# Expert outputs added to token rows in DRAM by accumulating indirect DMA, and a different order of the causal query tiles

## The chip, the core and the metric

The kernel runs on one core of one Trainium2 chip. A core has TensorE (PE in the profile, with the weight loads in a row of their own, PEld), VectorE (DVE), ScalarE (ACT), GpSimd (POOL) and SyncE (SP); each takes its instructions in program order and waits on semaphores. DMAs are issued by SP, ACT or POOL and are carried out by 16 DMA engines that all queues share. Time is device microseconds (us) for one execution, and the figure compared is the median over executions.

## The reference, cut to what matters

A two-layer decoder on `x` of 4 sequences x 512 tokens x 256 channels, with a context of 4 x 1024 x 128. Layer 0: a landmark attention, a causal self-attention with 16 heads plus a cross-attention to the context, and a linear layer with quantised operands. Layer 1: a hyperbolic attention, two attention blocks with an MLP each, and last a mixture of experts. Two parts matter here.

The causal attention of layer 0, 16 heads of width 16:

```python
att = jnp.einsum('bhqd,bhkd->bhqk', q, k) * scale
att = jnp.where(causal[None, None], att, -jnp.inf)
y = jnp.einsum('bhqk,bhkd->bhqd', jax.nn.softmax(att, axis=-1), v)
```

and the mixture of 8 experts, of which each token uses two:

```python
gate_scores = jax.nn.softmax(x @ Wg + bg, axis=-1)
topk_scores, topk_idx = jax.lax.top_k(gate_scores, TOP_K)
topk_scores = topk_scores / (jnp.sum(topk_scores, axis=-1, keepdims=True) + 1e-08)
...
for e in range(NUM_EXPERTS):
    h = jax.nn.gelu(x @ W1[e] + b1[e])
    y = h @ W2[e] + b2[e]
    output = output + y * combine_w[..., e:e + 1]
```

Here the `x` that enters the experts is a layernorm, and the result is added to the unnormalised `x`.

## The kernel before, in words

All arithmetic is in fp32 apart from a few bf16 helpers. `x` stays in SBUF as 16 tiles of 128 tokens from start to end. The stages follow each other in time as `l0_attn` and `context_T`, then `l0_xattn`, `l1_attn`, `l1_xattn`, and the experts (`Slots`), which begin while `l1_xattn` still runs.

*Order of the work.* The first two functions are ordered by a scheduler. From `l0_xattn` on the order is written by the kernel itself (`tc.manual_schedule()`): class `Stream` walks through steps. A step holds up to four "d" tiles (scores of one query tile for four heads, `d_tile`, L386; their row maxima on DVE, L394 for causal and L398 for full attention) and up to four "a" tiles of a unit some steps behind (transposed scores of one key tile, L421; exponentials on ACT, L422), and the products with the values (`outputs`, L517). In a step two d tiles and two a tiles are issued alternately, then the other two of each. The four heads of a unit lie in the four groups of 32 rows of the PE array. Everything else, such as projections, norms, the MLPs, the gate and the experts, hangs in `chains` of small pieces with a due step and a cost; `fill` lays them into the steps.

*Causal units.* A causal unit has four query tiles; tile `qt` needs (qt + 1) x 128 keys. `d_tile` takes them as `qt = NT - 1 - i`, so widths 512, 384, 256, 128 over its four steps. Key tile `kt` of an a tile needs the queries from kt x 128 on: widths 512, 384, 256, 128 as well. A unit's first a step lies ten steps after its first d step in the causal part, so that where both tiles of a step are causal, a step's d tile has index i + 2 (modulo 4) where its a tile has index i. Each of the four batches has 16 causal d steps; ten of them go with a tiles of a cross unit (always 512 wide) and six with causal ones.

*The gate.* For each batch, `gate` normalises `x` into `e.z` (a tile of the pool `z`), computes the scores, picks two experts (`choose`, `choose2`, `choose3`), counts each token's place within its expert (`rank`) and writes each token's normalised row twice, by `scatter`: eight indirect DMAs on POOL's queue (L1653) into the DRAM table `rows`, 2048 rows for each expert. Each of the eight waits for the one before it to land, since all of them write `rows`. `biases` and `biases2` add the experts' output biases, weighted, to `x`. `clear_rows` fills `rows` with zeros at the start of the kernel (L1554, 2 MB for each expert).

*The slots.* `NSLOT` = 39 slots of 128 rows each belong to one expert. Slots 0 to 15 (`NEARLY`) come from a table made after batch 2 (`table_early`), the others from one made after batch 3 (`table_late`). For a slot, `fetch_z` (L1803) loads 128 rows of `rows`, and `fetch_w` (L1809) loads one expert's whole weights, 2 MB, into one of four buffers; both are issued by SP after it has read the table. `turn` transposes the rows (L1820, L1822), `hidden` computes the first product (L1831) and the activation (L1833), `output` the second (L1838), which DVE copies out of PSUM to one of three `ys` buffers (L1840); SP stores it to the DRAM table `outs` (L1841). `round` fixes the order: fetch slot s+3, hidden s+1, turn s+2, output s. The second chain, `rest`, is made when batch 3 has been routed; its first piece is `fetch(16)`, which costs nothing in the planner and is therefore laid at once, among the fetches of slot 8. So on SP's queue stands the fetch of slot 16, rows first and then weights, ahead of the weights of slots 9 to 15, and its rows wait for the last scatter of batch 3.

*The end.* `places` (L1767 to L1794, on DVE, laid into the slots' work) computes for each token where its two results lie in `outs`. After the last slot, `end` gathers them: for each of the 16 token tiles two indirect DMAs on POOL's queue into `yk` (L1884), each followed by a multiply-add on DVE into `x` (L1887), and then a store of the tile on SP (L1888).

Of the kernel before, what the change touches and what calls it, by code (L numbers as in the profile page):

```python
# [13 lines left out]
I32 = mybir.dt.int32  # L14
# [16 lines left out]
VW = 16 * 17 + 15  # L31
NSLOT = 2 * B * T // P + E - 1

WROW = 2 * 1024 + 8 * C + 8
# [3 lines left out]
def decoder_kernel(ctx: ExitStack, tc: tile.TileContext, a: dict, out: bass.AP):  # L38
# [268 lines left out]
    class Stream:  # L307
# [70 lines left out]
        def d_tile(self, u, i, j):  # L378
            if u.mode == "causal":
                qt, hf = NT - 1 - i, 0  # L380
                n = (qt + 1) * P
            else:
                qt, hf, n = i // u.halves, i % u.halves, 512
            r = ts(j, 32)
            ps = ring()
            PE.matmul(ps[:, 0:n], u.qT[r, ts(qt)], u.kT[r, hf * 512 : hf * 512 + n], start=True, stop=True)  # L386
# [1129 lines left out]
    def moe_state(stack):  # L1516
        m = SimpleNamespace()
        pl = pool(stack, "moe", 1)
        dram = stack.enter_context(tc.tile_pool(name="moed", bufs=1, space=bass.MemoryType.DRAM))
        m.rows = dram.tile([E * B * T + P, C], F32, name="rows", tag="rows")  # L1520
        m.outs = dram.tile([NSLOT * P, C], F32, name="outs", tag="outs")
        m.wg = load(pl, "wg", rows("wg"), [P, 2, E])
# [15 lines left out]

        m.hot = pl.tile([P, 2, NTILE, E], BF16, name="hot", tag="hot")
        m.wt = pl.tile([P, 2, NTILE], F32, name="wt", tag="wt")  # L1540
# [9 lines left out]
    def clear_rows(m, pl):  # L1550
        zero = pl.tile([P, C], F32, name="zero", tag="zero")
        G.memset(zero, 0.0)
        for e in range(E):
            nc.sync.dma_start(  # L1554
                m.rows[ts(e, B * T), :].rearrange("(n p) c -> p n c", p=P), mid_bc(zero, B * T // P)
            )
        nc.sync.dma_start(m.rows[E * B * T :, :], zero)


    def gate(m, b, e, gs, hT, bank):  # L1560
# [8 lines left out]
        def z():  # L1569
            if not hasattr(e, "z"):  # L1570
                e.z = zpool.tile([P, NT, C], F32, name="ln_z", tag="ln_z")
            return e.z

        def begin():
            e.hT = hT()

        def flip(c):
# [16 lines left out]

        def top(mx, o):
            p, mc = e.p, t1("gmc")
            V.tensor_reduce(mx, p, AX.X, ALU.max)
            V.tensor_tensor(o, p, last_bc(mx, E), ALU.is_equal)
            V.tensor_mul(o, o, mid_bc(m.iw, NT))
            V.tensor_reduce(mc, o, AX.X, ALU.max)  # L1600
            V.tensor_tensor(o, o, last_bc(mc, E), ALU.is_equal)

        def choose():
            p = e.p
            e.o = [t8("go1"), t8("go2")]
            e.m2, e.sm = t1("gm2"), t1("gsm")
            V.tensor_reduce(e.sm, p, AX.X, ALU.add)
            V.reciprocal(e.sm, e.sm)
            V.tensor_mul(p, p, last_bc(e.sm, E))
            top(e.m1, e.o[0])  # L1610

        def choose2():
            p = e.p
            V.scalar_tensor_tensor(p, e.o[0], -2.0, p, ALU.mult, ALU.add)
            top(e.m2, e.o[1])

        def choose3():
# [4 lines left out]
            for k, mk in enumerate((e.m1, m2)):  # L1622
                V.tensor_mul(m.wt[:, k, ts(b, NT)], mk, sm)
                V.tensor_copy(m.hot[:, k, ts(b, NT), :], e.o[k])
            e.both = gs.tile([P, NT, E], BF16, name="gboth", tag="gboth")
# [24 lines left out]
        def scatter(t):  # L1650
            for k in range(2):
                i = b * NT + t
                G.indirect_dma_start(  # L1653
                    m.rows, bass.IndirectOffsetOnAxis(ap=m.idx[:, i, k : k + 1], axis=0), e.z[:, t, :], None
                )
# [13 lines left out]
        def biases2(h):  # L1669
            ps = bank()  # L1670
            for t in range(2):
                PE.matmul(ps[:, ts(t, C)], e.cT[:, ts(2 * h + t)], m.b2, start=True, stop=True)
            V.tensor_add(xb[:, ts(h, 2), :], ps.rearrange("p (t c) -> p t c", c=C), xb[:, ts(h, 2), :])

        return (
# [9 lines left out]
    class Slots:  # L1685
# [40 lines left out]
        def table(self, nm, nslot, end, less, plus):  # L1726
# [20 lines left out]
            V.tensor_copy(tab[:, 1, :], row)  # L1747
            return tab

        def table_early(self):  # L1750
            self.tab0 = self.table("tab0", NEARLY, self.end0, self.n0, None)

# [5 lines left out]
        def table_late(self):  # L1758
# [4 lines left out]

            self.tab1 = self.table("tab1", NSLOT - NEARLY, self.end1, less, n0[:, 0:1])


        def places(self):  # L1767
            m, one = self.m, self.st
            offs = []
            for nm, end, n, base in (("off0", self.end0, self.n0, 0), ("off1", self.end1, self.n1, NEARLY)):  # L1770
                off = self.t8(nm, E)
                V.tensor_sub(off, end, n)
                if base:
                    V.tensor_sub(off, off, self.n0)
                V.tensor_scalar(off, off, float(base), float(P), ALU.add, ALU.mult)
                V.tensor_sub(off, off, m.first)
                offs.append(off)
            V.tensor_sub(offs[0], offs[0], offs[1])
            lim = self.t8("lim", E)
            V.scalar_tensor_tensor(lim, self.n0, float(P), m.first, ALU.mult, ALU.add)  # L1780
            tmp = one.tile([P, NTILE, E], F32, name="tmp", tag="tmp")
            at, sel = (one.tile([P, NTILE], F32, name=n, tag=n) for n in ("slot", "early"))
            for k in range(2):
                V.tensor_mul(tmp, m.hot[:, k], mid_bc(lim, NTILE))
                V.tensor_reduce(sel, tmp, AX.X, ALU.add)
                V.tensor_tensor(sel, m.at[:, k, :], sel, ALU.is_lt)
                V.tensor_mul(tmp, m.hot[:, k], mid_bc(offs[0], NTILE))
                V.tensor_reduce(at, tmp, AX.X, ALU.add)
                V.tensor_mul(sel, sel, at)
                V.tensor_mul(tmp, m.hot[:, k], mid_bc(offs[1], NTILE))  # L1790
                V.tensor_reduce(at, tmp, AX.X, ALU.add)
                V.tensor_add(at, at, sel)
                V.tensor_add(at, at, m.at[:, k, :])
                V.tensor_copy(m.idx[:, :, k], at)  # L1794

# [3 lines left out]
        def fetch_z(self, u):  # L1799
            t, i = (self.tab0, u.s) if u.s < NEARLY else (self.tab1, u.s - NEARLY)  # L1800
            row = nc.sync.value_load(t[0:1, 1, i : i + 1], min_val=0, max_val=E * B * T)
            u.z = self.zp.tile([P, C], F32, name="zs", tag="zs")
            nc.sync.dma_start(u.z, self.m.rows[bass.ds(row, P), :])  # L1803
# [7 lines left out]
        def fetch(self, s):  # L1811
            u = self.us[s]
            if s >= NEARLY:
                self.fetch_z(u)
            self.fetch_w(u)

        def turn(self, u):
# [3 lines left out]
            u.zT = self.tp.tile([P, 2, P], F32, name="zsT", tag="zsT")  # L1821
            V.tensor_copy(u.zT, ps[:, 0:C].rearrange("p (c n) -> p c n", n=P))  # L1822

        def hidden(self, u, h):
# [10 lines left out]
        def output(self, u):  # L1835
# [3 lines left out]
            y = self.yp.tile([P, C], F32, name="ys", tag="ys")  # L1839
            V.tensor_copy(y, ps[:, 0:C])  # L1840
            nc.sync.dma_start(self.m.outs[ts(u.s), :], y)  # L1841

        def begin(self, stack):
            self.st = pool(stack, "l6c", 1)
            self.wp = pool(stack, "l6w", 4)
            self.zp = pool(stack, "l6z", NEARLY)
            self.tp = pool(stack, "l6t", 3)
            self.hp = pool(stack, "l6h", 2)
# [24 lines left out]
        def rest(self):  # L1873
            work = self.round(NEARLY - 3, NSLOT)
            work.insert(12, (0.5, self.places))
            return work


        def end(self):
            m = self.m  # L1880
            for i in range(NTILE):
                for k in range(2):
                    y = self.yp.tile([P, C], F32, name="yk", tag=f"yk{k}")
                    G.indirect_dma_start(  # L1884
                        y, None, m.outs, bass.IndirectOffsetOnAxis(ap=m.idx[:, i, k : k + 1], axis=0)
                    )
                    V.scalar_tensor_tensor(x[:, i, :], y, m.wt[:, k, i : i + 1], x[:, i, :], ALU.mult, ALU.add)  # L1887
                nc.sync.dma_start(out[i // NT, ts(i % NT), :], x[:, i, :])  # L1888

# [132 lines left out]
```

## Time and profile before

| | |
|---|---|
| median of 3 executions | 3517.08 us (3512.65 to 3517.96) |
| the profiled execution: its own time, and the span of its instructions | 3505.88 us, 3504.0 us |
| mean TensorE clock granted, of full speed | 0.914 |
| busy, share of the span: PE, PEld, DVE, ACT, POOL | 87%, 43%, 60%, 54%, 22% |
| weights of the slots: 39 loads of 2052 KB, issue to landing | 8.8 us (median) |
| store of a slot's output, 128 KB, issue to landing | 4.2 us (median) |
| scatter of 128 rows to `rows`, issue to landing | 2.4 us (median) |
| last product of the last slot ends, in the chain that ended last | about 3455 us |

How to read it: the page of a profile gives the busy time of each engine, and the chain of work that ended last, followed back from the last instruction. A busy share over the whole span is a mean over stages with different limits, so what a stage is bound by is read from that stretch. The profiled execution is one execution; it was 11 us faster than the median of the three others.

### The profile page before, as it was taken

How to read it: one execution, taken by the hardware profiler on the slowest of the kernel's cores; microseconds unless marked ns; L12 is line 12 of the kernel's file. 1: busy time of each engine (PE TensorE's matmuls, PEld its weight loads, DVE VectorE, ACT ScalarE, POOL GpSimd, SP SyncE). 2: the span in 40 equal slices, each digit the busy share in tenths (PEclk: the TensorE clock that was granted, in tenths of full speed). 3: DMA queues.
4: the chain of work that ended last, by engine and by line, in shares of the span. 5: the costliest groups of instructions: out<-in, count | busy, mean ns of one | idle time of the engine just before them, and what ended most of it. 6: DMA issues, size and time to landing. Idle time of an engine off the chain costs nothing.

```text
span 3504.0 us, 50650 instructions
## 1 busy us (share of the span) xinstructions
PE 3055.5 (87%) x19095; PEld 1489.4 (43%) x19095; DVE 2107.0 (60%) x5076; ACT 1901.9 (54%) x3845; POOL 781.5 (22%) x667
## 2 busy tenths in 40 slices
PE   6689999999998576677899999999998998987994
PEld 3433333333333344344434444433333333457894
DVE  4576676776765677876776565655646656532112
ACT  2235555454553865879587667465663655532231
POOL 1010112122022745677222121100102001011003
PEclk9789999999999567777899999999998999999997
DMA  8100000010001100110000000000000000045895
GB/s 281 59 24 7 1 7 3 6 31 4 11 19 41 56 1 32 54 69 7 25 1 1 1 19 1 7 13 19 13 1 13 7 1 19 1 164 208 290 328 168
DMA packets 81397, 176.08 MB, mean 50 GB/s; under 512 B 6264, under 2 KB 63744, under 8 KB 76032
## 3 DMA queue, kind: packets, MB, share of 16 engines
q1 hardware_dynamic: 76016, 161.16, 13.1%
q0 software_dynamic: 3072, 8.39, 0.8%
q8 instruction: 150, 2.46, 0.3%
q10 hardware_dynamic: 2064, 3.29, 0.3%
q14 instruction: 95, 0.78, 0.1%
HBM read 127.48 MB, written 45.34 MB: 49 GB/s over the span
## 4 chain that ended last, share of the span: by engine, by line
PE 66%; DVE 13%; ACT 7%; issue 7%; DMA 5%; POOL 2%; SPq 0%; ACTq 0%; DVEq 0%; POOLq 0%
PE ps_s L386 16%; PE ps_g L517 7%; PE ps_s L421 5%; PE ps_s L661 3%; PE ps_s L1831 3%; PE ps_s L1838 3%; PE ps_s L1410 3%; PE ps_s L1356 3%; PE ps_s L1426 3%; PE ps_s L414 2%; PE ps_s L1145 2%; PE ps_g L524 2%; DMA rows<-ln_z,idx 1%; PE ps_s L1367 1%; DMA we<-in_we 1%
## 5 line engine op out<-in xcount | busy, mean ns | idle before, releaser
L422 ACT ACTIVATE pt<-ps_s 128x512 f32<-128x512 f32 (+2 forms) x1536 | 791.0, 569 | 749.0 <-PE ps_s L421 647.8
L386 PE MATMUL ps_s<-kT,qT 32*128 32x512 f32 (+3 forms) x3072 | 921.9, 623 | 45.6 <-ACT pt L422 28.0
L398 DVE TENSOR_REDUCE mx<-ps_s 128x1 f32<-128x512 f32 x768 | 489.3, 683 | 222.0 <-PE ps_s L386 124.8
L386 PEld LDWEIGHTS ps_s<-kT,qT 32*128 32x128 f32 x3072 | 310.9, 186 | 338.5 <-issue 96.4
L390 DVE TENSOR_REDUCE mx<-ps_s 128x1 f32<-128x512 f32 x512 | 328.3, 684 | 194.1 <-PE ps_s L386 190.9
L421 PE MATMUL ps_s<-qa,kT 32*128 32x512 f32 (+3 forms) x1536 | 436.0, 590 | 4.9 <-ACT pt L422 3.1
L421 PE MATMUL ps_s<-qT,kT 32*128 32x512 f32 x1536 | 417.6, 636 | 0.0
L402 ACT ACTIVATE ps_s<-ps_s,mx 128x512 f32<-128x512 f32 x512 | 340.9, 670 | 32.8 <-DVE mx L390 32.3
L1833 ACT ACTIVATE hid<-ps_s,we 128x128 f32<-128x128 f32 x312 | 88.9, 368 | 221.4 <-PE ps_s L1831 144.5
L1105 POOL TENSOR_TENSOR s<-s,mh 128x1280 f32<-128x1280 f32 x64 | 187.1, 2948 | 76.9 <-ACT mh L1104 57.1
L394 DVE CUSTOM_DVE_ANT_0 junk<-ps_s,dmask 128x512 f32<-128x512 f32 (+3 forms) x256 | 125.2, 489 | 95.8 <-PE ps_s L386 52.9
L1831 PE MATMUL ps_s<-zsT,we 128*128 128x128 f32 x1248 | 148.8, 278 | 22.7 <-DMA we<-in_we 20.6
L1088 PE MATMUL ps_s<-qk 32*128 32x256 f32 (+3 forms) x512 | 105.3, 628 | 65.6 <-DVE mh L1093 55.3
L421 PEld LDWEIGHTS ps_s<-qa,kT 32*128 32x128 f32 x1536 | 143.8, 185 | 42.7 <-DVE mx L398 24.0
L414 PE MATMUL ps_s<-qm,all 3*128 3x512 bf16 x768 | 156.6, 387 | 5.8 <-ACT ps_s L402 3.1
L164 POOL TENSOR_TENSOR ln_r<-ln_ve,mhalf 128x4 f32<-128x4 f32 x40 | 40.8, 1020 | 538.4 <-DVE ln_ve L159 476.0
L1831 PEld LDWEIGHTS ps_s<-zsT,we 128*128 128x128 f32 x1248 | 146.5, 194 | 28.0 <-issue 19.2
L1120 POOL TENSOR_TENSOR s<-s 128x1280 f32<-128x1280 f32 x64 | 147.6, 2337 | 12.3 <-ACT s L1116 12.3
L1147 DVE COPY pt<-ps_s 128x512 f32<-128x512 f32 x160 | 108.3, 687 | 58.7 <-PE ps_s L1145 58.7
L1145 PE MATMUL ps_s<-ident,s 128*128 128x128 f32 x640 | 127.7, 336 | 16.6 <-ACT s L1139 15.3
L1838 PE MATMUL ps_s<-we,hid 128*128 128x256 f32 x624 | 141.0, 379 | 0.0
L1093 DVE TENSOR_SCALAR_CACHE_REDUCE mh<-ps_s 128x512 f32<-128x512 f32 (+3 forms) x256 | 108.5, 486 | 53.1 <-PE ps_s L1092 28.8
(439 smaller groups left out, 5117.5 us busy)
## 6 DMA issues: line engine op xcount, KB each, us to landing
we<-in_we SPq DMA_DIRECT2D x39, 2052.0 KB, 8.8
rows<-zero SPq DMA_DIRECT2D x8, 2048.0 KB, 16.8
qk_d<-qkT SPq DMA_DIRECT2D x32, 256.0 KB, 2.7
qk<-qk_d SPq DMA_DIRECT2D x8, 1024.0 KB, 6.5
zs<-rows SPq DMA_DIRECT2D x39, 128.0 KB, 3.6
outs<-ys SPq DMA_DIRECT2D x39, 128.0 KB, 4.2
li<-in_a_li SPq DMA_DIRECT2D x4, 1024.0 KB, 8.7
v_d<-vp SPq DMA_DIRECT2D x16, 143.5 KB, 1.8
```

Source lines behind the costliest of these rows:

```text
L386: PE.matmul(ps[:, 0:n], u.qT[r, ts(qt)], u.kT[r, hf * 512 : hf * 512 + n], start=True, stop=True)
L390: V.tensor_reduce(m, ps[:, 0:n], AX.X, ALU.max, negate=True)
L398: V.tensor_reduce(m, ps[:, 0:n], AX.X, ALU.max)
L402: S.activation(ps, ps, AF.Exp, bias=m, accum_out=sm)
L414: PE.matmul(ps, self.ones[r, :], u.qm[r, :], start=True, stop=False)
L421: PE.matmul(ps[:, c0:], u.kT[r, ts(kt)], (u.qa if u.first_row else u.qT)[r, c0:], start=u.first_row, stop=True)
L422: S.activation(u.pt[:, j, c0:], ps[:, c0:], AF.Exp, scale=u.scale)
L517: PE.matmul(o[r, c0:], u.v(kt, j), pt[:, j, c0:], start=first, stop=last)
L1105: G.tensor_add(s, s, m)
L1145: PE.transpose(ps[:, ts(j)], u.s[h // 2][:, h % 2, c0 : c0 + P], ident)
L1831: PE.matmul(ps[:, ts(f)], u.w[:, k : k + P], u.zT[:, c, :], start=c == 0, stop=c == 1)
L1838: PE.matmul(ps[:, 0:C], u.h[:, f, :], u.w[:, 2048 + f * C : 2048 + f * C + C], start=f == 0, stop=f == 7)
```

## The change

Rows carry four more numbers. `rows` gets `RW` = 260 columns: the token's number, its second weight, the difference of its two weights, and a mark that says which expert is its first. The gate writes them into its own tile `gz`, of the pool `l5g`, which takes the place of `e.z`; cleared rows get the number of a spare row. A slot then knows its rows' tokens and weights: `turn` has three more small DVE instructions, and `output` multiplies by the weight as it copies out of PSUM.

The results are summed in DRAM. A new table `sums` has one row for each token and 128 spare rows. After `biases2` POOL writes the batch's `x` into it, and each slot adds its 128 weighted rows by one indirect DMA on POOL's queue that accumulates. The program orders these DMAs: each waits for the one before it to land. `outs`, its stores, `places` and the gathers are gone; `end` copies `sums` to `out` by four DMAs from DRAM to DRAM, two on SP's queue and two on ACT's.

The fetch of slot 16 takes the weights first and then the rows. The causal query tiles are taken as 1, 0, 3, 2, so that widths are 256, 128, 512, 384. The buffers for the turned rows grow from three to four, since `turn`'s new small tiles are in the same pool.

The program's order on POOL's queue around batch 3 becomes: the adds of slots 0 to 4, the constants for the late table, the eight scatters, the add of slot 5, the write of batch 3 into `sums`, and the other 33 adds. On SP's queue the stores of `outs` are missing, and nothing else moves but slot 16's weights.

```diff
+RW = C + 4
...
-                qt, hf = NT - 1 - i, 0
+                qt, hf = (1 - i) % NT, 0
...
-        m.rows = dram.tile([E * B * T + P, C], F32, name="rows", tag="rows")
-        m.outs = dram.tile([NSLOT * P, C], F32, name="outs", tag="outs")
+        m.rows = dram.tile([E * B * T + P, RW], F32, name="rows", tag="rows")
+        m.sums = dram.tile([B * T + P, C], F32, name="sums", tag="sums")
...
+        num = pl.tile([P, NTILE + 1], I32, name="numi", tag="numi")
+        G.iota(num, pattern=[[P, NTILE + 1]], base=0, channel_multiplier=1)
+        m.num = pl.tile([P, NTILE + 1], F32, name="num", tag="num")
+        V.tensor_copy(m.num, num)
...
-        zero = pl.tile([P, C], F32, name="zero", tag="zero")
+        zero = pl.tile([P, RW], F32, name="zero", tag="zero")
         G.memset(zero, 0.0)
+        V.tensor_copy(zero[:, C : C + 1], m.num[:, NTILE:])
...
+        nc.sync.dma_start(m.sums[B * T :, :], zero[:, 0:C])
...
-                e.z = zpool.tile([P, NT, C], F32, name="ln_z", tag="ln_z")
+                e.zr = gs.tile([P, NT, RW], F32, name="gz", tag="gz")
+                e.z = e.zr[:, :, 0:C]
...
+            V.tensor_copy(e.zr[:, :, C], m.num[:, ts(b, NT)])
...
-                V.tensor_copy(m.hot[:, k, ts(b, NT), :], e.o[k])
+            V.tensor_copy(e.zr[:, :, C + 1], m.wt[:, 1, ts(b, NT)])
+            V.tensor_sub(e.zr[:, :, C + 2], m.wt[:, 0, ts(b, NT)], m.wt[:, 1, ts(b, NT)])
...
+            if h:
+                G.dma_start(m.sums[ts(b, T), :].rearrange("(t p) c -> p t c", p=P), xb)
...
-        def places(self):
...
         def fetch(self, s):
             u = self.us[s]
+            if s == NEARLY:
+                self.fetch_w(u)
             if s >= NEARLY:
                 self.fetch_z(u)
-            self.fetch_w(u)
+            if s != NEARLY:
+                self.fetch_w(u)
...
+            mark = self.mark0[:, u.s : u.s + 1] if u.s < NEARLY else self.mark1[:, u.s - NEARLY : u.s - NEARLY + 1]
+            u.to = self.tp.tile([P, 1], I32, name="to", tag="to")
+            V.tensor_copy(u.to, u.z[:, C : C + 1])
+            u.wt = self.tp.tile([P, 1], F32, name="wts", tag="wts")
+            V.tensor_tensor(u.wt, u.z[:, C + 3 : C + 4], mark, ALU.is_equal)
+            V.scalar_tensor_tensor(u.wt, u.wt, u.z[:, C + 2 : C + 3], u.z[:, C + 1 : C + 2], ALU.mult, ALU.add)
...
-            V.tensor_copy(y, ps[:, 0:C])
-            nc.sync.dma_start(self.m.outs[ts(u.s), :], y)
+            V.tensor_scalar_mul(y, ps[:, 0:C], u.wt)
+            G.indirect_dma_start(
+                self.m.sums, bass.IndirectOffsetOnAxis(ap=u.to, axis=0), y, None, compute_op=ALU.add
+            )
...
-            self.tp = pool(stack, "l6t", 3)
+            self.tp = pool(stack, "l6t", 4)
...
-            work.insert(12, (0.5, self.places))
...
         def end(self):
-            m = self.m
-            for i in range(NTILE):
-                for k in range(2):
-                    y = self.yp.tile([P, C], F32, name="yk", tag=f"yk{k}")
-                    G.indirect_dma_start(
-                        y, None, m.outs, bass.IndirectOffsetOnAxis(ap=m.idx[:, i, k : k + 1], axis=0)
-                    )
-                    V.scalar_tensor_tensor(x[:, i, :], y, m.wt[:, k, i : i + 1], x[:, i, :], ALU.mult, ALU.add)
-                nc.sync.dma_start(out[i // NT, ts(i % NT), :], x[:, i, :])
+            for b in range(B):
+                (nc.scalar if b % 2 else nc.sync).dma_start(out[b], self.m.sums[ts(b, T), :])
```

More of the change, by code (lines that the diff above doesn't have):

```diff
@@ L1537, in moe_state @@
         )
-        m.hot = pl.tile([P, 2, NTILE, E], BF16, name="hot", tag="hot")
+        num = pl.tile([P, NTILE + 1], I32, name="numi", tag="numi")
+        G.iota(num, pattern=[[P, NTILE + 1]], base=0, channel_multiplier=1)
+        m.num = pl.tile([P, NTILE + 1], F32, name="num", tag="num")
+        V.tensor_copy(m.num, num)
         m.wt = pl.tile([P, 2, NTILE], F32, name="wt", tag="wt")
@@ L1592, in scores, with top @@
             S.activation(e.p, e.p, AF.Exp)
-        def top(mx, o):
-            p, mc = e.p, t1("gmc")
+        def top(mx, o, mc):
+            p = e.p
             V.tensor_reduce(mx, p, AX.X, ALU.max)
@@ L1609, in choose @@
             V.tensor_mul(p, p, last_bc(e.sm, E))
-            top(e.m1, e.o[0])
+            top(e.m1, e.o[0], e.zr[:, :, C + 3])
         def choose2():
@@ L1614, in choose2 @@
             V.scalar_tensor_tensor(p, e.o[0], -2.0, p, ALU.mult, ALU.add)
-            top(e.m2, e.o[1])
+            top(e.m2, e.o[1], t1("gmc"))
         def choose3():
@@ L1653, in scatter @@
                 G.indirect_dma_start(
-                    m.rows, bass.IndirectOffsetOnAxis(ap=m.idx[:, i, k : k + 1], axis=0), e.z[:, t, :], None
+                    m.rows, bass.IndirectOffsetOnAxis(ap=m.idx[:, i, k : k + 1], axis=0), e.zr[:, t, :], None
                 )
@@ L1747, in table @@
             V.tensor_copy(tab[:, 1, :], row)
-            return tab
+            mark = self.t8(nm + "m", nslot)
+            V.tensor_scalar(mark, ex, -1.0, float(E), ALU.mult, ALU.add)
+            return tab, mark
         def table_early(self):
-            self.tab0 = self.table("tab0", NEARLY, self.end0, self.n0, None)
+            self.tab0, self.mark0 = self.table("tab0", NEARLY, self.end0, self.n0, None)
         def count_late(self):
@@ L1762, in table_late @@
             V.tensor_sub(less[:, 0 : E - 1], less[:, 0 : E - 1], n0[:, 1:E])
-            self.tab1 = self.table("tab1", NSLOT - NEARLY, self.end1, less, n0[:, 0:1])
-        def places(self):
[L1768 to L1782, printed above, removed]
-            for k in range(2):
[L1784 to L1794, printed above, removed]
+            self.tab1, self.mark1 = self.table("tab1", NSLOT - NEARLY, self.end1, less, n0[:, 0:1])
         def go(self):
@@ L1801, in fetch_z @@
             row = nc.sync.value_load(t[0:1, 1, i : i + 1], min_val=0, max_val=E * B * T)
-            u.z = self.zp.tile([P, C], F32, name="zs", tag="zs")
+            u.z = self.zp.tile([P, RW], F32, name="zs", tag="zs")
             nc.sync.dma_start(u.z, self.m.rows[bass.ds(row, P), :])
@@ L1839, in output @@
             y = self.yp.tile([P, C], F32, name="ys", tag="ys")
-            V.tensor_copy(y, ps[:, 0:C])
-            nc.sync.dma_start(self.m.outs[ts(u.s), :], y)
+            V.tensor_scalar_mul(y, ps[:, 0:C], u.wt)
+            G.indirect_dma_start(
+                self.m.sums, bass.IndirectOffsetOnAxis(ap=u.to, axis=0), y, None, compute_op=ALU.add
+            )
         def begin(self, stack):
-            self.st = pool(stack, "l6c", 1)
             self.wp = pool(stack, "l6w", 4)
             self.zp = pool(stack, "l6z", NEARLY)
-            self.tp = pool(stack, "l6t", 3)
+            self.tp = pool(stack, "l6t", 4)
             self.hp = pool(stack, "l6h", 2)
@@ L1873, in rest @@
         def rest(self):
-            work = self.round(NEARLY - 3, NSLOT)
-            work.insert(12, (0.5, self.places))
-            return work
+            return self.round(NEARLY - 3, NSLOT)
         def end(self):
-            m = self.m
-            for i in range(NTILE):
-                for k in range(2):
-                    y = self.yp.tile([P, C], F32, name="yk", tag=f"yk{k}")
-                    G.indirect_dma_start(
-                        y, None, m.outs, bass.IndirectOffsetOnAxis(ap=m.idx[:, i, k : k + 1], axis=0)
-                    )
-                    V.scalar_tensor_tensor(x[:, i, :], y, m.wt[:, k, i : i + 1], x[:, i, :], ALU.mult, ALU.add)
-                nc.sync.dma_start(out[i // NT, ts(i % NT), :], x[:, i, :])
+            for b in range(B):
+                (nc.scalar if b % 2 else nc.sync).dma_start(out[b], self.m.sums[ts(b, T), :])
     moe = moe_state(ctx)
```

## The prediction

> **What bounds the kernel now.** I read the page first, then busy times by stretch, then the chain that ended last in order of time, then TensorE's timeline in one causal stretch. The page says that the whole is a TensorE kernel:
>
> ```profile
> PE 66%; DVE 13%; ACT 7%; issue 7%; DMA 5%; POOL 2%; SPq 0%; ACTq 0%; DVEq 0%; POOLq 0%
> ```
>
> But the change lies mostly in the last 10% of the span, where the limits differ (columns: stretch, length, busy us and counts for PE, PEld, DVE, ACT, POOL; then clock, DMA share, GB/s):
>
> ```profile
> 3182.00:3227.00 45.00, 27.10 (x176) 24.13 (x174) 11.11 (x44) 6.84 (x24) 7.64 (x8) 0.89 0.57 218
> 3227.00:3292.00 65.00, 61.10 (x400) 55.88 (x400) 11.99 (x46) 18.25 (x64) 0.00 (x0) 0.97 0.72 258
> 3300.00:3448.00 148.00, 148.00 (x1030) 139.74 (x1029) 17.26 (x41) 46.79 (x164) 0.00 (x0) 1.00 0.86 311
> 3455.00:3504.00 49.00, 0.21 (x1) 0.00 (x0) 15.92 (x33) 0.00 (x0) 30.29 (x32) 0.55 0.47 131
> ```
>
> From 3300 PE is full, but the 16 DMA engines are at 0.86 as well. In the last 49 us PE does nothing. The chain tells what each stretch waits for (start, length, what):
>
> ```profile
> 3189.12 5.23 DMA rows<-ln_z,idx
> ...
> 3194.62 2.41 DMA rows<-ln_z,idx
> ...
> 3209.00 2.40 DMA rows<-ln_z,idx
> ...
> 3214.26 12.49 DMA we<-in_we
> 3226.89 5.67 PE ps_s L1831 x32
> ...
> 3284.73 0.42 DVE ys L1840
> 3286.63 0.30 DVE tmp L1784
> ...
> 3291.86 0.42 DVE zsT L1822
> 3292.32 3.84 PE ps_s L1831 x32
> ...
> 3455.70 1.68 DMA outs<-ys
> ...
> 3496.99 2.84 DMA yk<-outs,idx
> ```
>
> So: the scatters of batch 3, one after the other; a 12.5 us wait for weights behind them; at 3285 `places` on DVE, with PE waiting for a turned tile behind it; and the 32 gathers at the end.
>
> **The change part by part.** The sum is against the span of 3504.0 us.
>
> *The end.* The last product ends at 3455.2. Now follow 48.8 us: the store of slot 38, 32 gathers 1.25 us apart, multiply-adds and stores. Instead there comes: the scaled copy, 0.4 (L1840's 0.42); the last add; the copy to `out`. Nearest row for an add: a scatter, 0.96 on POOL, 2.40 to landing, issue included. The one ahead (slot 37, ready 3.5 us earlier) delays it little. An accumulating DMA isn't in the trace: it also reads its destination, so I take 3.5 to 4; below is 2.4 (no such work is less than a plain scatter), above some 8. The copy: 2 MB, read and written. Nearest row: the clearing DMAs of 2 MB, which go out 5.75 us apart in the first 60 us; with the 2 us a small DMA takes to land, 8. Sum 0.4 + 4 + 8 + 1 for the issue = 13.4. Gain **35.4 us**, ends 28 and 38.
>
> *`places`* goes. PE stood from 3284.7 to 3292.3 behind its DVE instructions (6.7 us, 3285.15 to 3291.86). The next slot's weights were already there, since they are slot 16's. Without `places` the turned tile is made at once. Late next: slot 17's weights, issued at 3279 and 8.5 us on the way, still in time. Gain **6.5**, ends 3 and 7.
>
> *Causal widths.* On TensorE's timeline (start, length):
>
> ```profile
> 371.13 0.48 PE L386 MATMUL ps_s<-kT,qT 32*128 32x256 f32 x1
> 371.13 0.69 PE L421 MATMUL ps_s<-qa,kT 32*128 32x512 f32 x1
> ...
> 372.20 1.06 PE L517 MATMUL ps_g<-pt,vc 128*32 128x512 f32 x8
> ...
> 384.70 0.58 PE L386 MATMUL ps_s<-kT,qT 32*128 32x384 f32 x1
> 384.70 0.37 PE L421 MATMUL ps_s<-qa,kT 32*128 32x128 f32 x1
> ...
> 385.55 0.64 PE L517 MATMUL ps_g<-pt,vs 128*32 128x256 f32 x8
> ```
>
> A d and an a tile start together, so the row groups run side by side, and the next work starts when the wider one is through: 1.07 us for a half step of 512 and 256, 0.85 for 384 and 128, hence 0.21 per 128 columns of the wider one. Before, the six doubly causal steps of a batch have widest tiles 512, 384, 512, 384, 512, 384; after, 512, 384, 256, 128, 512, 384. That is four units of 128 less, twice per step: 8 x 0.21 = 1.7 us a batch, 6.8 in all. The ten steps beside cross tiles keep 512. PE is 902 of 925 us busy in this stage, so this counts; but steps of 512 and 512 now load DVE (four maxima at 0.84 us) and ACT at once. I take **6**, ends 0 and 7.
>
> *The adds on POOL's queue.* Each add waits for its `ys` and for the landing of the one before; behind it on POOL wait the norm's power, the table's constants and the scatters. The row first: the scatter at 3189.12, issued 3 us after a 2 MB weight load, took 5.23 us; those with no load under way took 2.40. The adds of slots 3 and 4 come ready at 3177.5 and 3184.9, each beside a weight load. So add 3 lands at about 3187, add 4 is issued by 3188, and the first scatter comes at 3189 instead of 3181.9. It lands behind the load of 3186, near 3194, as the second one does now. Then slot 16's weights, now fetched early (about 3198, when slot 5 frees its buffer), hold up one scatter by 5 us. Slot 16's rows go out near 3218 instead of 3211.4. Against this, slot 9's weights no longer stand behind 2 MB for slot 16: they need 8.3 from 3219, not 12.5 from 3214.3. Both arrive at about 3227: **0**.
> [...] The trace has the 5.23, so I go by the row; ends -9 and +12.
>
> *The slots from 3227.* Removed for each slot: a 128 KB store on SP (4.2 us, hidden). Added: an add on POOL, 0.96 and some 4 to 9 to land. With three `ys` buffers, the product of slot s+3 needs add s landed; a slot takes 7.24 us, so an add may take 7.24 on average. If it lands with the weight load ahead of it, it still lands once per slot, since there is one load per slot. The DMA engines: 2.36 MB in 7.24 us at share 0.9 is 6.5 us; the add moves 0.13 MB once more to read its destination, some 0.4 us. It fits, narrowly: **+1**, ends 0 and +15. DVE's three small instructions per slot (about 0.17 us each, as L1743) lie in an engine busy 12%.
>
> *Batch 2.* The write of `x` (0.5 MB, 1 us on POOL) stands before the MLP's addition at 3091.65 and before slot 0's weights, for which PE waits until 3109.7: 0.5 MB at the 366 GB/s that three loads reached from 3213 to 3232 is 1.4 us. **+1.5**, ends 0 and +4.
>
> *Wider rows.* Clearing writes rows of 1040 bytes. By the row, 2 MB per 5.75 us, 1.6% more is 0.7 us. [...]
>
> Sum: -35.4 - 6.5 - 6 + 0 + 1 + 1.5 + 1 = -44.4, span about 3460. The profiled execution took 3505.9, 11 us less than the median 3517.1; I take the difference off the median: 3473, rounded up to **3475** as not all parts will come whole.
>
> **The rivals.** *A: as above*, 0.62, between 3464 and 3484.
> *B: the adds load the DMA engines.* An add then costs each engine 1 us or so more than the store did; 6.5 + 1.1 exceeds 7.24, slots go to about 7.8, 23 slots cost 13, and the scatters' delay comes at its upper end, 10. Net about -22: 3495. For it: shares of 0.86, and landings of 8 us beside loads. Against: only 6% more bytes. 0.22.
> *C: the chain of adds becomes the bound, and it is slower.* Place: POOL's queue, from slot 5's add at about 3215 on. 34 adds follow one another; the end stays at 3504 if the last lands by 3495, so it decides at (3495 - 3215) / 34 = 8.2 us from add to add. If reading the destination, adding and writing take a second pass behind the weights, 9.5 us, the last lands at 3538 and the span is 3547: 43 more, 3560. For it: stores issued just behind weights did take over 8 us to land. Against: such a delay comes once per slot, and slower slots leave the DMA engines room. 0.12.
> *D: the causal order brings nothing*, since the maxima are the bound in the wide steps: 6 less than A, 3481. I count it in A. That the adds merge with nothing at all, 0.04: 3517.
>
> **How the numbers follow.** This kernel's executions lie within about 0.2%, 7 us: less than that can't be told from no change. A and B are faster: 0.84. Slower is C, 0.12, and 0.04 remain for same. The range has A, most of B and half of what lies between B and no change: 3458 to 3506; the upper part of B and C are left out, about 0.18.
>
> **What would show it.** Right: the span ends about 13 us after the last L1838; no idle PE before slot 16's first product; slots 7.2 to 7.3 us apart, POOL waiting for DVE and not for its own DMAs; landing of adds 3 to 6 us; in steps of 256 and 256, L517 0.64 after the first tile. Wrong: DVE's scaled copy waiting for a `ys` buffer (C), slots 7.6 us or more apart at a DMA share near 1 (B), rows of slot 16 later than about 3225, or clearing that runs past 100 us.

## The result, and the profile after

The changed kernel's median is 3480.26 us (3474.72 to 3491.11, 6 runs) against 3514.19 us for the kernel before on the same chip: ratio 0.9911, 95% interval 0.9887 to 0.9935. The profiled executions say less: span 3481.7 us against 3504.0, so 22.3 us. The execution profiled before was 8 us faster than its median here, the one profiled after 3 us slower than its own. The parts below are compared between those two spans.

The chain that ended last is another one now. By engine and by line, from the page of the changed kernel:

```profile
DMA 5%; DVE 0%; issue 0%; POOLq 0%
DMA sums<-ys,to 5%; DVE wts L1821 0%; DVE to L1818 0%; DVE wts L1820 0%; POOLq L2008 0%; DVE ys L1839 0%; POOLq L1840 0%
```

Before it held 66% of TensorE. Now it runs back over adds only, with DVE's short steps between them, and TensorE isn't in it. The two shares can't be compared, since the walk back stops at 3256.5 us here: it tells of slot 10's add and what follows, and of nothing ahead of it. By stretch (length, busy us and counts for PE, PEld, DVE, ACT, POOL; clock, DMA share, GB/s):

```profile
3182.00:3227.00 45.00, 27.63 (x163) 24.87 (x164) 11.24 (x48) 5.70 (x20) 10.30 (x11) 0.81 0.53 189
3227.00:3285.00 58.00, 54.20 (x366) 50.04 (x365) 9.24 (x36) 17.10 (x60) 12.41 (x8) 1.00 0.83 269
3285.00:3440.00 155.00, 145.46 (x967) 136.01 (x966) 22.34 (x95) 43.34 (x152) 29.32 (x19) 0.97 0.88 295
3464.00:3482.00 18.00, 0.00 (x0) 0.00 (x0) 0.40 (x1) 0.00 (x0) 2.94 (x2) 0.60 0.46 131
```

The stretch without TensorE at the end has shrunk from 49 us to 18. The stretch that had TensorE full, 148 of 148, now has 145 of 155. The place is seen in the timeline (start, length, engine, line, what; in brackets the idle time before it and what ended it):

```profile
3371.28 1.54 POOL L1840 DMA_INDIRECT sums<-ys,to  x1 [7.11 <-DVE wts L1821]
...
3381.47 0.15 DVE L1818 CAST to<-zs 128x1 int32<-128x1 f32 x1 [9.70 <-DMA sums<-ys,to]
...
3382.18 1.54 POOL L1840 DMA_INDIRECT sums<-ys,to  x1 [9.36 <-DVE wts L1821]
3382.26 0.41 DVE L1814 COPY zsT<-ps_s 128x256 f32<-128x256 f32 x1
3382.73 5.21 PE L1830 MATMUL ps_s<-zsT,we 128*128 128x128 f32 x32 [2.55 <-DVE zsT L1814]
```

An add holds its token numbers (`to`, in SBUF) until it has landed, and `to` has four buffers. So the turn of slot s+4 writes `to` only after the add of slot s has landed: DVE's 9.70 us before 3381.47 are such a wait. Behind `to` stand, in DVE's order in the program, the weights, the scaled copy of a finished slot, and the next turned tile (3382.26). The scaled copy is what POOL needs for the next add, and the turned tile is what TensorE needs. It is a loop: an add lands, 0.7 us later the next one goes out. The chain view shows one round of it:

```profile
3371.28 10.17 DMA sums<-ys,to
...
3381.47 0.15 DVE to L1818
3381.63 0.08 DVE wts L1820
...
3381.73 0.23 DVE wts L1821
...
3382.18 8.06 DMA sums<-ys,to
```

The waits from 3285 to 3455 (us in total, times, longest):

```profile
DVE to L1818 <- DMA sums<-ys,to: 142.0, 22, 10.3
DVE zsT L1814 <- PE ps_s L1812: 2.9, 3, 1.7
...
PE ps_s L1830 <- DVE zsT L1814: 9.5, 3, 4.0
```

DVE waits for adds in 142 of these 170 us; TensorE waits for DVE in 9.5 of them, in three waits, the first at 3380. From slot 6's add at 3227.4 to slot 38's at 3468.3 there are 32 steps, 7.53 us each on average. While weights are loaded they are longer, 7.93 us up to slot 32's add at 3433.6; the last three, without loads, are 4.4. TensorE needs 7.24 us a slot (the first products at 3271.35 and 3278.59 of this trace). By slot 28 the slack is used up, and from there to slot 33 TensorE loses 15.2 us (five slots took 51.47 instead of 36.23).

Where the 22.3 us come from, as differences of the two traces:

| stretch | before | after | difference |
|---|---|---|---|
| to the first maximum of `l0_xattn` | 200.7 | 202.5 | +1.8 |
| from there to its last causal maximum | 880.4 | 872.4 | -8.0 |
| to slot 0's second product | 2032.5 | 2031.1 | -1.4 |
| slot 0 to slot 8 | 119.0 | 121.2 | +2.2 |
| slot 8 to slot 16 | 63.6 | 62.4 | -1.2 |
| slot 16 to the end of the last product | 159.0 | 174.3 | +15.3 |
| from there to the end of the span | 48.8 | 17.8 | -31.0 |

The first line is scatter: over all kernels run here it was 199.1 to 202.5. So is the third: in two kernels of the experiments below (caus_only and places_spread), which have the old code in that stretch, it took 2035.7 and 2041.5.

### The profile page after: what moved, and what is told of

Same layout as the page of the kernel before. It is cut to its first block, busy times and chain, and to the rows that moved or that the text cites. A ratio compares the mean times of both kernels' runs of the same rounds, so it can differ in the third digit from the quotient of the medians.

```text
span 3481.7 us, 50606 instructions
## 1 busy us (share of the span) xinstructions
PE 3066.6 (88%) x19095; PEld 1497.5 (43%) x19095; DVE 2092.8 (60%) x5138; ACT 1902.4 (55%) x3845; POOL 815.4 (23%) x679
## 5 line engine op out<-in xcount | busy, mean ns | idle before, releaser
L398 DVE CUSTOM_DVE_ANT_0 junk<-ps_s,dmask 128x256 f32<-128x256 f32 (+3 forms) x256 | 125.6, 491 | 92.0 <-PE ps_s L425 40.3
L1149 PE MATMUL ps_s<-ident,s 128*128 128x128 f32 x640 | 130.5, 341 | 16.5 <-ACT s L1143 15.3
```

Of the source, the lines that this page charges most:

```text
L1149: PE.transpose(ps[:, ts(j)], u.s[h // 2][:, h % 2, c0 : c0 + P], ident)
```

## The experiments

They were timed in four groups, on four chips, each against the kernel before. Differences between kernels are told by medians, with each kernel's ratio to the kernel before. The changed kernel was timed in none of these groups, and the kernel before had a median of 3514.2 us in the changed kernel's own group and of 3509.1 to 3511.0 in these. So gains against the changed kernel are 1 to 4 us smaller by ratios than by medians, and its own interval is 8 us to each side.

### Does the chain of adds hold TensorE?

**deep**: more buffers, the same chain.

```diff
-            u.to = self.tp.tile([P, 1], I32, name="to", tag="to")
+            u.to = self.kp.tile([P, 1], I32, name="to", tag="to")
...
-            u.wt = self.tp.tile([P, 1], F32, name="wts", tag="wts")
+            u.wt = self.kp.tile([P, 1], F32, name="wts", tag="wts")
...
-            self.yp = pool(stack, "l6y", 3)
+            self.yp = pool(stack, "l6y", 6)
+            self.kp = pool(stack, "l6k", 8)
```

> The changed kernel with more buffers around the adds: six for ys instead of three, and eight of their own for to and wts instead of four. Theory (the adds' chain holds DVE through the buffers of to, and DVE holds TensorE): the five gaps between slots 28 and 33, 15 us of TensorE, go, the last product ends near 3449 instead of 3464. The adds are still one chain, 7.5 us apart while weights are loaded and 3.7 after, so the last lands near 3462: 8 to 10 us faster than the changed kernel, about 43 less than the kernel before. Rival 1 (the weights come late, the DMA engines are full): the gaps stay, within 2 us of the changed kernel. Rival 2 (the landings alone set the end, whatever the buffers): TensorE ends at 3449, but the last add lands at 3470 as it did, 0 to 2 us.

Measured: 3471.62 us, ratio 0.9888 (0.9871 to 0.9904), 9 us less than the changed kernel by medians; the two intervals overlap, so the reading rests on the traces. Slots are 7.2 us apart from slot 14 to slot 36, and the last product ends at 3442.9. The end of its chain:

```profile
3435.95 6.92 PE ps_s L1837 x32
3443.41 3.82 DMA sums<-ys,to
3447.96 3.60 DMA sums<-ys,to
```

The gaps are gone, so the buffers did hold TensorE. This kernel widens `ys` as well as `to`; that it was `to` is read from the changed kernel's trace, where DVE waits for adds at `to` and never for a buffer of `ys`. But the end came forward by only 16 us in the span where TensorE came forward by 21 us: the last add waits in a queue of adds and lands at 3456.0, 13 us after the last product. The adds were 7.7 us apart while weights were loaded (slot 6 at 3221.2 to slot 32 at 3422.4) and 4.3 to 5.2 apart at the end. Rival 1 falls; rival 2 was half true.

**plain**: scatters that don't accumulate.

```diff
-                self.m.sums, bass.IndirectOffsetOnAxis(ap=u.to, axis=0), y, None, compute_op=ALU.add
+                self.m.sums, bass.IndirectOffsetOnAxis(ap=u.to, axis=0), y, None
```

> The changed kernel with plain scatters in place of accumulating ones: the results overwrite the tokens' rows, so the sum is left out. Same bytes written, the destination isn't read. Theory (it is the accumulation that makes an add dear: 1.54 us on POOL instead of 0.96, 3.7 alone instead of 2.4): add to add falls to 6 us or so, no gaps in slots 28 to 33, TensorE ends at 3449, then one add of 2.4 and the copy: 15 to 18 us faster than the changed kernel. Rival (an add is slow because it stands beside the weight loads, whatever it does at its end): add to add stays over 7 us, gaps stay, 2 to 4 us faster.

Measured: 3459.73 us, ratio 0.9861 (0.9845 to 0.9877), 20 us less than the changed kernel, no gaps. Its POOL, the group of the scatters over the kernel (least, median and longest ns) and what POOL waits for from 3285 to 3440:

```profile
L1840 POOL DMA_INDIRECT sums<-ys,to x39: 954/958/1086, 3109.8 to 3444.9; - x39
```
```profile
POOL sums L1840 <- DMA sums<-ys,to: 125.2, 20, 8.0
POOL sums L1840 <- DVE ys L1839: 5.4, 1, 5.4
```

The issue costs 0.96 us instead of 1.54, and alone a scatter lands in 2.4 us instead of 3.7. But beside weight loads it needs much longer too, often 6 to 8 us. From slot 6 to slot 37 the landing was 6.0 us on average, 6.8 in the changed kernel and 6.5 in deep, where TensorE has no gaps either. So the greater part of an add's time is the weights that it stands beside; the accumulation adds 0.5 to 0.8 us on this average and 1.3 alone. That part decides all the same: from slot 14 to slot 32 the scatters went out 7.24 us apart, which is TensorE's own pace, and the adds of deep 7.66. The theory's "6 us or so, add to add" was too low: each scatter still waited for the one before. The rival was right that the loads make an add slow, and wrong that the gaps would stay.

**two**: two chains, same work.

```diff
+        m.odd = dram.tile([B * T + P, C], F32, name="odd", tag="odd")
...
+        nc.sync.dma_start(m.odd.rearrange("(n p) c -> p n c", p=P), mid_bc(zero[:, 0:C], B * T // P + 1))
...
-                self.m.sums, bass.IndirectOffsetOnAxis(ap=u.to, axis=0), y, None, compute_op=ALU.add
+                self.m.odd if u.s % 2 else self.m.sums, bass.IndirectOffsetOnAxis(ap=u.to, axis=0), y, None, compute_op=ALU.add
```

> The changed kernel with two tables: the odd slots add into a second table, cleared at the start and left out of the output (so half of the experts' results is missing). Each add now waits for the add before the last to land, and the work for the DMA engines is the same. Theory (the wait of each add for the one before is what binds): no gaps, TensorE ends at 3449, the last add lands by 3454, span near 3463, 17 to 20 us faster than the changed kernel. Rival (the DMA engines are full): gaps stay, within 3 us.

Measured: 3462.41 us, ratio 0.9865 (0.9849 to 0.9880), 18 us less than the changed kernel. Groups of POOL from 3227 to 3420 (busy us, mean ns, then idle time before them and what ended it):

```profile
L1842 POOL DMA_INDIRECT sums<-ys,to x13 | 20.1, 1544 | 77.4 <-DVE ys L1841 77.4
L1842 POOL DMA_INDIRECT odd<-ys,to x13 | 20.1, 1542 | 76.9 <-DVE ys L1841 69.9 <-DMA sums<-ys,to 7.0
```

POOL waits for results now, not for its own DMAs. The adds are as dear as before, dearer even (9 to 10 us to land with two in flight), but nobody waits. TensorE ran at 7.24 us a slot with a DMA share of 0.93 from 3285 to 3440: the DMA engines weren't the bound. And the tail behind the last product was 14.1 us, where the prediction's sum had 13.4.

### What the order of the causal query tiles is worth

**caus_back**: the changed kernel with the old order.

```diff
-                qt, hf = (1 - i) % NT, 0
+                qt, hf = NT - 1 - i, 0
```

> The changed kernel with the old order of causal query tiles (512, 384, 256, 128). By the doubly causal steps in the two traces the new order gained 3.9 us: 4 us slower than the changed kernel. The prediction's step said 6. Rival (maxima on DVE set the wide steps): 0.

Measured: 3480.98 us, ratio 0.9923 (0.9908 to 0.9938): 0.7 us more than the changed kernel by medians and 4 by ratios, a difference that these runs can't tell from none or from a few us. Yet its stage was 877.3 us long, where all kernels with the new order have 872.4 to 876.5 and the others with the old one 880.4 to 880.6, and slot 8's second product came 6 us later than in the changed kernel. The last product ended 1 us earlier all the same. The adds stood 7.36 us apart instead of 7.53, and TensorE lost 6.6 us in one gap there instead of 15.2, nearly all of it in three. Where the chain sets the end, time won ahead of it can be lost in it. Two kernels without the chain as the bound decide.

**two_old** (two tables, old order) and **caus_only** (the kernel before, new order; the diff turned round):

> The kernel with two tables (the odd slots' results left out of the output) and the old order of causal query tiles. With one chain of adds the old order cost nothing in the whole (3481.0 us against 3480.3), though its stage was 5 us longer. Theory (the chain of adds swallowed it, as it sets the end from slot 8 on): without the chain as the bound the old order costs its 5 to 6 us, near 3468 against 3462.4. Rival (the order is worth nothing, the stage's 5 us are noise or come back later): within 1.5 us of 3462.4.

> The kernel before with the new order of causal query tiles alone. No chain of adds stands behind it. Theory: 5 us faster than the kernel before, as between two_old and two. Rival: the order's gain is real only together with the changed slots, 0.

Measured: 3467.35 us for two_old, ratio 0.9881 (0.9867 to 0.9896), 4.9 us more than two, with no overlap of the runs (3466.13 to 3471.16 against 3460.85 to 3464.28). And 3503.04 us for caus_only, ratio 0.9983 (0.9974 to 0.9992), so 6 us less than the kernel before (3 to 9). The order is worth 5 to 6 us wherever the end hangs on TensorE. That it works as the prediction had it is seen in the changed kernel's steps of 256 and 256 (start, length):

```profile
383.65 0.48 PE L390 MATMUL ps_s<-kT,qT 32*128 32x256 f32 x1
383.65 0.48 PE L425 MATMUL ps_s<-qa,kT 32*128 32x256 f32 x1
...
384.29 0.85 PE L521 MATMUL ps_g<-pt,vs 128*32 128x384 f32 x8
```

The next work starts 0.64 us after the first tile, where a half step of 512 and 256 took 1.07.

### What places cost

**places_spread**: the kernel before, with `places` in seven pieces.

```diff
-            work.insert(12, (0.5, self.places))
+            for n, f in enumerate(self.places()):
+                work.insert(25 + 6 * n, (0.1, f))
```

> The kernel before with places cut into seven pieces, laid one per slot or so from slot 18 on; the same instructions. The prediction's step: places holds TensorE for 6.5 us, so 6.5 us faster than the kernel before. Rival (by the timeline TensorE worked through it, and waited 0.4 to 0.8 us for the turned tile at 3292.3): 0.7 us faster, not to be told from no change.

Measured: 3511.94 us, ratio 1.0007 (0.9998 to 1.0016). It gains nothing, or 0.7 us at the most. What the prediction should have looked at is the timeline of the kernel before at that place:

```profile
3284.53 3.73 PE L1831 MATMUL ps_s<-zsT,we 128*128 128x128 f32 x32
...
3285.07 0.16 DVE L1772 TENSOR_TENSOR off<-endE,n 128x8 f32<-128x8 f32 x1
...
3288.32 3.62 PE L1838 MATMUL ps_s<-we,hid 128*128 128x256 f32 x16
...
3291.85 0.42 DVE L1822 COPY zsT<-ps_s 128x256 f32<-128x256 f32 x1
...
3292.32 3.84 PE L1831 MATMUL ps_s<-zsT,we 128*128 128x128 f32 x32 [0.39 <-DVE zsT L1822]
```

While DVE computed the places, TensorE did a whole slot's two products, and then waited 0.39 us.

### The fetch of slot 16

**two_zfirst**: two tables, rows before weights as before the change.

```diff
-            if s == NEARLY:
-                self.fetch_w(u)
             if s >= NEARLY:
                 self.fetch_z(u)
-            if s != NEARLY:
-                self.fetch_w(u)
+            self.fetch_w(u)
```

> The kernel with two tables (odd slots' results left out of the output), but slot 16's rows fetched before its weights, as before the change. The prediction put the new order, with what it does to the scatters of batch 3, at 0 between -9 and +12. By the traces slot 0 to slot 8 took 119.0 us before and 121.2 after, and slot 9's weights landed at 3226.8 and 3221.4. Theory (the weights of slot 9 are what TensorE waits for at 3227, and they now come earlier, as slot 16's no longer stand between): the old order is 3 to 6 us slower, near 3467. Rival (the early weights hold up a scatter by 5 us and so the rows: nothing gained): within 1.5 us of 3462.4.

Measured: 3462.50 us, ratio 0.9867 (0.9852 to 0.9882), the same as two. The expected 3 to 6 us weren't there: the prediction's 0 holds.

**deep_inturn** and **two_inturn**: the fetch of slot 16 isn't laid at once but after slot 14's first product, so it is behind the other slots' weights on SP's queue. Both also take the fetch back to its old form, rows before weights.

```diff
-            return self.round(NEARLY - 3, NSLOT)
+            work = self.round(NEARLY - 3, NSLOT)
+            work.insert(2, work.pop(0))
+            return work
```

> The kernel with deeper buffers, and the fetch of slot 16 laid after the first product of slot 14 instead of at once: it no longer stands on SP's queue ahead of the weights of slots 9 to 15, nor takes one of four weight buffers while slots 9 to 15 run. TensorE was busy 27.6 of the 45 us from 3182 to 3227, so its work can end some 12 us earlier. Theory (one chain of 34 adds, 7.5 us each, starts behind batch 3's scatters and sets the end, whatever TensorE does): 0 to 4 us faster than 3471.6. Rival (TensorE sets the end): 10 to 14 us faster, near 3460.

> The kernel with two tables (odd slots' results left out of the output) and the fetch of slot 16 in its turn. Here the adds don't bind. Theory: slots 8 to 16 start some 12 us earlier and the whole is 10 to 14 us faster than 3462.4, near 3450. Rival (the DMA engines are full from slot 8 on, so earlier weights only crowd the others): less than 4 us.

Measured for deep_inturn: 3471.12 us, ratio 0.9890 (0.9868 to 0.9913), the same as deep (3471.62). Its stretches:

```profile
3182.00:3227.00 45.00, 41.89 (x265) 38.17 (x266) 10.90 (x43) 10.49 (x37) 11.59 (x11) 0.90 0.69 242
...
3285.00:3440.00 155.00, 144.30 (x980) 135.29 (x978) 24.96 (x97) 44.40 (x156) 33.26 (x22) 0.98 0.83 272
3440.00:3500.00 60.00, 0.00 (x0) 0.00 (x0) 0.00 (x0) 0.00 (x0) 5.35 (x4) 0.77 0.18 44
```

TensorE is busy 41.9 us of the 45 from 3182 to 3227, where it was 34.5 in deep and 27.6 in the changed kernel. It ends at 3429.3, 13.6 us earlier than in deep, and the span doesn't move (3465.8 against 3465.6): in both kernels the last add lands at 3456.0. This is the plainest sign that one chain of adds sets the end.

Measured for two_inturn: 3457.37 us, ratio 0.9848 (0.9835 to 0.9860), 5 us less than two, where 10 to 14 were expected. DVE's waits from 3205 to 3240 say why:

```profile
DVE to L1817 <- DMA odd<-ys,to: 24.1, 1, 24.1
DVE to L1817 <- DMA sums<-ys,to: 5.1, 1, 5.1
```

Slot 5's add stands on POOL's queue behind batch 3's scatters, and with four buffers of `to` slot 9's turn can't be finished before it has landed. The early weights are of no use then: slot 8 to slot 9 took 25.5 us. The wait had only moved.

### All together

**best**: deeper buffers, two tables, slot 16 in turn, complete. Odd slots up to 31 go to the second table, and this adds it to the first:

```diff
+            if u.s == 32:
+                both = [d[0 : B * T, :].rearrange("(a b) c -> a (b c)", b=4) for d in (self.m.sums, self.m.odd)]
+                G.dma_start(both[0], both[1], accum_op=ALU.add, max_dma_last_dim=4096)
```

> All of it together, complete: six buffers for ys and eight for to and wts; odd slots up to 31 add into a second table, which one accumulating DMA (2 MB, DRAM to DRAM) adds to sums behind slot 32's add; slot 16 fetched in its turn. TensorE should end near 3429, as with one chain and that fetch order. Theory (two chains keep pace with 7.24 us a slot): slot 32 ends near 3390, the merge moves 6 MB and takes some 15 us until 3408, six adds at 4.4 us follow, the last lands near 3435, the copy ends near 3444: 3446, 25 us faster than one chain with deep buffers (3471). Rival (the merge is slow, as it reads two tables and stands beside the weights: 30 us or more): the last add lands at 3450 or later, 3460 and above.

Measured: 3458.65 us, ratio 0.9858 (0.9843 to 0.9873). TensorE ends at 3425.4 and every slot from slot 6 to slot 36 takes 7.2 us. But the chain ends so:

```profile
3386.19 10.47 DMA sums<-ys,to
3397.97 21.16 DMA sums<-odd
3419.89 3.73 DMA sums<-ys,to
```

The merge took 21.2 us, between the theory's 15 and the rival's 30, and five more adds follow those shown. It is now the bound.

**best2**: no merging DMA. The second table takes the odd slots up to 35; SP loads it into `x`'s tiles behind slot 36, and DVE adds both at the end.

```diff
+            if u.s == 36:
+                for b in range(B):
+                    nc.sync.dma_start(x[:, ts(b, NT), :], self.m.odd[ts(b, T), :].rearrange("(t p) c -> p t c", p=P))
...
+            for b in range(B):
+                q[b % 2].dma_start(y[:, ts(b, NT), :], self.m.sums[ts(b, T), :].rearrange("(t p) c -> p t c", p=P))
             for b in range(B):
-                (nc.scalar if b % 2 else nc.sync).dma_start(out[b], self.m.sums[ts(b, T), :])
+                V.tensor_add(x[:, ts(b, NT), :], x[:, ts(b, NT), :], y[:, ts(b, NT), :])
+                q[b % 2].dma_start(out[b].rearrange("(t p) c -> p t c", p=P), x[:, ts(b, NT), :])
```

> As the last complete version (two tables, deeper buffers, slot 16 in its turn), but the second table isn't added by a DMA, which took 21.2 us in the chain of adds there. Odd slots up to 35 add into it; behind slot 36's output SP loads it into the dead tiles of x, while the weights' loads are over. At the end SP and ACT load sums into a free weight buffer by batches, DVE adds, and both store to out. Theory (the merge was all that stood between the last product, 3425, and the end): two chains end near 3431, the load of 2 MB takes 8 us, add and store of the last batch 1.6 and 3: near 3445, so 3447 and 10 to 12 us faster than 3458.7. Rival (the adds of the two chains lag the products by far more when TensorE never waits): the last add at 3440 or later, no gain.

Measured: 3449.16 us, ratio 0.9832 (0.9814 to 0.9850): 60 us less than the kernel before, and 31 less than the changed one by medians (28 by ratios). One stretch, and the end of its chain:

```profile
3227.00:3420.00 193.00, 193.00 (x1338) 182.15 (x1337) 33.18 (x131) 61.07 (x215) 46.90 (x31) 1.00 0.96 319
```
```profile
3424.21 3.59 DMA sums<-ys,to
3428.53 3.69 DMA sums<-ys,to
3432.69 7.94 DMA we<-sums
```

TensorE is full for 193 us at a DMA share of 0.96, and ends at 3426.2; the last add lands 6 us later.

## Why the prediction was right, and where it wasn't

The predicted 3475 lies 5 us from the measured 3480, and the direction and the main part were right. But of the terms of its sum two failed by more than 5 us, and the sum against the span, 44.4 us, was twice the 22.3 that the two spans show.

- *The end*, -35.4: right in its working. It came to -31.0. An add alone landed in 3.7 us (3.5 to 4 was taken), the copy with its issue took 9.6 us (9 was taken). What was missed is that the last add isn't alone: those of slots 36 and 37 are late too, so that it goes out at 3468.3 only and lands 8.2 us after the last product. Without that queue, in two, the tail was 14.1 us, which makes -34.7.
- *places*, -6.5: wrong, it is 0 to -0.7. The step read the DVE lines in the chain view as time in which TensorE stood. The chain shows one engine at a time; that DVE is in it doesn't mean that TensorE is idle. The timeline of the same kernel had "0.39" in the brackets, and places_spread gained nothing.
- *Causal widths*, -6: right, and so rival D falls. The half steps of 256 and 256 took the 0.64 us that was named as a sign. The stage was 8.0 us shorter between the two traces, caus_only gained 6 us and two_old lost 5. Not all of it is traced to its place: the doubly causal steps alone gave 3.9 us, as the expectation of caus_back says. In the changed kernel that gain can't be seen in the whole.
- *The adds on POOL's queue*, 0: the sum was right (+2.2 from slot 0 to slot 8, and the order of slot 16's fetch worth nothing). The row, 5.23 us for a scatter beside a load, was the right guide: in plain the scatters took 2.4 us alone and often 6 to 8 beside SP's weights, and the changed kernel's adds 3.7 alone and 6.8 on average. The lower end, -9, has no row behind it and no run shows it: slot 0 to slot 8 became 2.2 us longer.
- *The slots from 3227*, +1: wrong, it was +14 to +15. "An add may take 7.24 on average", "it fits, narrowly" is where it failed: an add took 6.8 us to land on average, and 0.7 more went by before the next was issued, which the step left out. Together 7.53; while weights are loaded 7.93 (7.73 in deep, without TensorE's gaps), which is 0.5 to 0.7 over the limit, 26 times over. The step also named the wrong buffer. It counted the three of `ys`, but the four of `to` bind a round earlier, since a turn stands two slots ahead of an output.
- *Batch 2*, +1.5: open. The stretch up to slot 0 was 1.4 us shorter, but it scatters by more than that (2032.5 to 2041.5 with the old code).
- *Wider rows*, +1: no run shows this term by itself. The median scatter took 2.5 us from issue to landing instead of 2.4, and the eight clearing DMAs landed 6.41 us apart on average instead of 5.93 (the step took one interval, 5.75), 8% more, with 1.6% more bytes. The last of them landed at 78 us, ahead of the loads at 103, so that was hidden.

Of the rivals, B named full DMA engines: refuted, as two and best2 ran 7.24 us a slot at shares of 0.93 and 0.96. C named the chain of adds: its mechanism is what happened. Its price wasn't: it turned the sign from 8.2 us an add on, and the chain took 7.53 (7.7 from slot 5's add on, where C began to count). So C cost some 15 us in the slots and 4 at the end, and not 43. The signs didn't part A from C: POOL did wait for DVE and not for its own DMAs, as A had it (134.7 us for `wts`), but DVE in turn waited for those DMAs; and C's sign, a wait for a `ys` buffer, never came, as the wait was at `to`.

That the forecast was so near is in part luck. The terms were too good by 22 us in all, 20 of them in two. Half of that was made up because the sum was taken off the median, and the profiled execution lay 11 us below it; the 11 us were a property of that execution and not of the kernel. Against its own fresh runs the kernel gained 34 us by medians, 23 to 40 by the interval.

## What to carry to other kernels

A row of DMAs that each wait for the one before has a pace of landing plus issue (6.8 + 0.7 us for the adds here), and it has to be compared with the pace of the work as a rate: 0.5 to 0.7 us too slow for each of 26 slots is 13 to 18 us, and buffers only put off when it is paid. Count the buffers of everything that such a DMA reads, its index tile too, and ask what stands behind their next writer on that engine. And before a stall is priced from a chain view, look at the bound engine's own line in the timeline: idle time in brackets is the price, with what a slower clock adds behind it (1.5 to 1.7 us after each of the three waits here), and not the length of what the chain lists. When an experiment frees the bound engine and the end doesn't move, as with deep_inturn, the bound is named.

## What was not expected of the hardware

*Three waits of 2.55 to 4.00 us cost TensorE more than their length.* Around the wait of 2.55 us at 3380 (PE's busy us, then clock, DMA share, GB/s):

```profile
3381.00:3382.70 1.70, 0.00 (x0) 0.86 1.06 284
3382.70:3384.00 1.30, 1.27 (x6) 0.50 1.01 430
3384.00:3386.00 2.00, 2.00 (x13) 0.59 0.95 369
3386.00:3388.00 2.00, 2.00 (x21) 1.00 0.89 293
```

The granted clock falls to a half and stays there, by these rows, for about 0.5 + 1.3 + 1.6 = 3.4 us, most of it after the wait is over; the 32 products took 5.21 us instead of 3.73. For the three waits of this kind in the changed kernel (2.55, 2.99 and 4.00 us) that is 5 of the 15 us lost (5.21, 5.47 and 5.46 us for the 32 products behind them). The waits for weights at 3238, 3254 and 3263, of 1.31, 1.53 and 0.96 us, left the clock at 1.00.

*The adds cost POOL and the DMA engines more than plain scatters.* An indirect DMA of 128 rows of 1 KB took 1.54 us to issue when it accumulates and 0.96 when it doesn't, and 3.7 and 2.4 us to land alone. The DMA share from 3285 to 3440 was 0.89 in deep and 0.83 in plain. One accumulating DMA of 2 MB from DRAM to DRAM took 21.2 us, where the plain copy of 2 MB at the end was through in 9.6 us, issue included; but the copy came after the last product, and the other went out at 3398, 27 us before it, so how much of the difference is the adding stays open.
